# Moving bias, weighting and one sum between engines in the last two batches of a gathered attention kernel, with a new written-out order

## The chip, the core and the metric

The kernel runs on one core of a Trainium2 chip. The metric is device time in microseconds (us) of one execution. Three timed runs of the kernel before took 1618.98, 1622.75 and 1625.38 us, so the median is 1622.75 us. One further execution was recorded by the profiler: it took 1612.02 us, and its span from the first to the last instruction is 1609.9 us.

Engine names: PE is TensorE (matmul), DVE is VectorE, ACT is ScalarE, POOL is GpSimd (it also issues the indirect gathers), SP is SyncE (it only issues transfers).

## The reference

The input x has 16 batches of 1024 rows of 512 numbers. An adjacency matrix of 1024 x 1024 zeros and ones, the same for all batches, says which rows a row may look at; most rows have only a few neighbours and itself.

```
h   = max(layernorm(x), 0)
q   = h @ Wq + bq ;  k = h @ Wk + bk ;  v = h @ Wv + bv     # 8 heads of 64
s   = q.k / sqrt(64) + (0 where adj, -1e9 elsewhere)
out = x + softmax(s) @ v
```

## The kernel before

**Tiling.** The rows are sorted by their number of neighbours and cut into 8 tiles of 128 rows, t = 7 (fewest) to t = 0 (most). Per batch and tile, x is loaded, normalised (`norm`, ACT), transposed on PE (`flip`), copied to SBUF (`unflip`, ACT), multiplied by Wk and Wv (`proj_kv`, PE), copied out of PSUM (`evict_kv`) and stored to a table of K and V rows in DRAM (`store_kv`, SP). A row's K and V are then fetched slot by slot, one neighbour per slot and row, with indirect gathers (`gather`, POOL); slot 0 of a tile is the row itself and comes by a plain transfer (SP).

**Units.** The slots of a batch are worked off in 14 units u0 to u13 of 2 to 4 slots. u0 is (7,0), meaning tile 7 from slot 0; u6 is (2,0), u7 (2,3), u8 (1,0), u9 (1,4), u10 (0,0), u11 (-1,0) (further pieces of long rows), u12 (0,4), u13 (0,8). For each unit: `multiply` by q (L1298) and `score` (L1302) on DVE, `exponent` (L1306) on ACT, then each slot's V row is weighted: by `weigh_v` on DVE (one instruction, L1318), by `weigh_s` on ACT (8 instructions, one per head, L1332), or by `weigh_p` on POOL. `fold` (L1337) and `join` (L1344) sum slots on DVE or POOL; for tile 0, and for most tiles of the last batch, PE sums them in PSUM (`add_up`, L1356). `scale` divides by the row sum, `residual` (L1406) adds x, `put_out` (L1409, POOL) writes the rows. Tile 0's q is also copied to SBUF by `copy_q` (ACT, L1279), from which PE makes the q of u11 (`queries` of tile -1).

**Who adds the bias.** PE adds a bias by one more matmul into the same PSUM tile (L1055). For the V of tiles t = 7, 5, 3, 1 of every batch but the first it doesn't: DVE adds the bias while copying out of PSUM (L1073). All other copies out are ACT's (L1075).

**The order.** There is no run-time scheduling. A planner (`planned`, `Plan.ordered`) lists all operations with their engine, what each must follow and the buffers it uses. A table `PLACES` holds a number for each operation of a batch; an engine's operations are issued in the order of place plus 95.290021 times the batch number. Batches 0, 1 and 2 have tables of their own, batches 3 to 13 share one, the next to last (14) and the last (15) have `next` and `last`. `once` and `first` hold the preparation. Places only order; each engine works its list in that order and waits where something is missing. Known dependencies in the planner serve the order in which the code is written; waits on the chip come from the real uses of buffers.

**Buffers.** There are 6 gather buffers (`g`), used in turn, 2 PSUM tiles for K and V (`pkv`), 2 for q, 2 for sums (`acc`), 2 for transposes and 3 tiles for K and V on the way to DRAM. The last batch takes its units in the order 10, 11, 12, 13, 8, 6, 9, 7, 4, 3, 5, 2, 1, 0.

**Overlap of batches.** While PE makes the K and V of batch b, DVE, ACT and POOL do the attention of batch b - 1. All gathers of batch b need all eight `store_kv` of batch b.

Of the kernel before, what the change touches and what calls it, by code (L numbers as in the profile page):

```python
# [70 lines left out]
NT = len(CAPS)  # L71
BY_VECTOR = {2: 1, 3: 0, 4: 1}
ONE_MORE = ((2, 0),)
LAST_BY_VECTOR = {(2, 0): 0, (2, 3): 0, (0, 0): 0, (-1, 0): 0, (3, 0): 0, (1, 4): 0}
VECTOR_RESIDUAL = (4,)
LAST_VECTOR_RESIDUAL = (5, 4, 6, 7)
# [21 lines left out]
        list_of=(-13.2, -13.4, 13.93, 14.05, -4.33, -7.76, -9.88, 14.25,),  # L98
        tell=(-12.63, -16.97, -13.14, 9.24, 0.89, 16.11, 17.75, 19.88,),
        spread=(45.38, 47.45, 30.7, 45.48, 45.35, 30.46, 22.54, 45.26,),  # L100
        collect=(-9.17, 5.02,),
        others=(14.42,),
        perm_of=(0.42,),
        spots=(26.84,),
        long_rows=(30.4,),
        long_blocks=(16.58, 20.59, 22.61, 24.22, 24.98,),
        longest=(27.18, 29.37, 32.28, 35.43, 36.11, 39.52, 41.52, 44.79, 45.14,),
        count_pieces=(46.89,),
        first_piece=(122.72,),
        owners=(94.07,),  # L110
        flip_owners=(136.43,),
        copy_owners=(113.68,),
        list_pieces=(137.27,),
        pieces=(127.38,),
        slots=(142.24,),
        add_bias=(-19.2, -17.6,),
        spread_bias=(68.07,),
        copy_bias=(89.7,),
# [4 lines left out]
        norm=(75.49, 76.09, 77.09, 77.49, 79.89, 80.09, 80.34, 80.69,),  # L123
        flip=(75.49, 75.69, 76.49, 76.69, 78.69, 78.89, 90.39, 104.64,),
        unflip=(75.89, 76.49, 77.29, 77.89, 80.49, 80.72, 96.22, 97.88,),
        proj_kv=(75.89, 77.49, 76.29, 77.89, 76.89, 78.49, 79.09, 79.29, 86.87, 98.15, 99.79, 107.75, 135.06, 147.6, 153,
            148.32,),
        evict_kv=(76.89, 79.29, 77.69, 79.49, 78.09, 80.29, 80.4, 80.66, 96.1, 96.13, 96.42, 106.28, 154.55, 162.49, 169.71,
            172.46,),
        store_kv=(78.35, 116.17, 119.38, 125.35, 140.7, 146.55, 148.18, 147.06,),  # L130
        variance=(75.89, 76.89, 79.29, 81.69,),
        power=(75.69, 76.29, 78.29, 87.8,),
# [3 lines left out]
        load_x=(30.09, 30.5, 38.8, 45.21, 45.44, 47.92, 49.07, 49.69,),  # L136
        norm=(2.13, 2.31, 24.77, 49.09, 71.39, 77.14, 77.27, 78.66,),
        flip=(50.32, 51.95, 54.11, 55.9, 60.64, 67.45, 67.52, 68.48,),
        unflip=(27.69, 53.06, 72.64, 77.2, 79.54, 81.13, 82.77, 84.23,),
        queries=(67.49, 69.07, 115.56, 126.07, 127.49, 138.29, 148.67, 168.76, 169.97,),  # L140
        gather=(45.09, 65.92, 63.96, 81.66, 82.98, 67.8, 87.05, 86.63, 69.01, 87.14, 102.98, 103.26, 67.61, 108.86, 109.63,
            108.64, 107.92, 79.49, 116.69, 119.1, 130.36, 131.45, 130.44, 102.76, 142.21, 138.67, 142.4, 144.98, 150.63,
            142.37, 142.46, 108, 152.91, 152.09, 152.7, 153.37, 153.1, 152.82, 153.23, 171.08, 171.84, 155.19, 172.79,
            155.41, 171.17, 171.11,),
        multiply=(47.46, 64.59, 81.01, 107.03, 126.74, 113.33, 126.77, 141.63, 149.43, 155.18, 163.45, 170.22, 180.88,
            178.07,),
        score=(47.54, 67.41, 96.06, 111.76, 129.2, 117.87, 128.06, 146.83, 153.31, 155.84, 165.66, 174.39, 181.78, 195.93,),
        exponent=(92.19, 93.82, 105.44, 111.15, 115.51, 115.42, 115.56, 141.97, 143.4, 152.67, 166.31, 172.53, 173.27,
            183.23,),
        row_sums=(64.37, 70.18, 97.04, 118.27, 142.77, 160.52, 163.48, 203.64,),  # L150
        share=(64.49, 74.75, 101.56, 119.16,),
        weigh_v=(69.44, 130.54, 142.01, 144.6, 161.03, 163.57, 170.25, 175.36, 195.82,),
        weigh_s=(92.85, 101.83, 100.44, 95.75, 106.78, 112.94, 106.75, 115.48, 115.39, 115.45, 122.29, 116.89, 121.19, 119.7,
            142.94, 135.53, 142.97, 143.03, 144.58, 154.99, 152.31, 153.27, 163.13, 166.52, 165.91, 171.8, 172.93, 171.74,
            173.08, 173.04, 172.99, 174.92, 175.62, 181.86, 185.22, 185.42, 187.44,),
        fold=(71.91, 97.01, 97.07, 132.47, 137.68, 138.95, 141.69, 143.23, 145.64, 143.05, 153.79, 155.15, 156.82, 161,
            163.76, 171.2, 173.85, 175.66, 181.17, 186.5, 187.92, 183.84, 200, 202.21, 204.35, 204.53,),
        residual=(109.25, 124.53, 138.45, 141.77, 153.19, 171.14, 178.55, 219.35,),
        put_out=(129.95, 130.51, 141.35, 142.43, 153.4, 178.16, 179.5, 225.23,),
        join=(147.89, 161.06, 175.01,),  # L160
        scale=(148.16, 161.67, 176.53, 211.41,),
        copy_q=(145.23,),
        add_up=(188.54, 194.88, 203.87, 205.55,),
        more=(201.41,),
        pass_on=(203.77,),
        seen=(331.72,),
    ),
    1: dict(
        load_x=(-45.57, -43.85, -39.73, -39.1, -35.32, -8.38, 7.1, 14.11,),
        stats=(-63.36, -61.71, -54.75, -49.26, -50.34, -20.16, 1.69, 45.35,),  # L170
        norm=(-12.29, -8.07, -1.29, 11.92, 17.92, 21.28, 45.19, 45.66,),
        flip=(-14.6, 13.76, 33.62, 50.55, 65.56, 72.21, 73.87, 79.53,),
        unflip=(-6.21, -2.22, 15.4, 21.31, 28.65, 37.54, 57.61, 68.73,),
        proj_kv=(17.02, 20.04, 31.75, 42.81, 49.67, 52.6, 71.12, 55.79, 72.24, 74.1, 74.46, 79.5, 79.61, 83.24, 86.3, 90.4,),
        evict_kv=(-2.01, -35.87, 14.8, 20.07, 20.47, 37.41, 38.89, 36.39, 47.71, 60.13, 57.69, 63.79, 70.59, 76.3, 77.5,
            77.55,),
        store_kv=(7.84, 6.03, 7.72, 17.75, 21.65, 22.37, 41.88, 46.5,),
        variance=(-59.83, -48.24, 0.42, 46.54,),
        power=(-31.44, 7.33, 34.59, 50.93,),
        shift=(-56.77, -25.47, 22.23, 52.69,),  # L180
        queries=(92.98, 95.46, 99.76, 113.88, 114.01, 119.61, 134.23, 135.77, 151.42,),
        gather=(53.63, 85.6, 64.02, 85.49, 85.7, 72.03, 102.18, 95.44, 87.81, 104.49, 108.17, 108.68, 107.7, 109.8, 109.4,
            111.58, 112.73, 107.63, 119.79, 126.28, 135.9, 135.96, 135.93, 140.28, 147.73, 148, 149.33, 149.5, 150.8, 150.83,
            149.71, 142.94, 156.83, 157.14, 151.75, 157.7, 150.86, 150.89, 162.73, 165.24, 165.07, 165.98, 165.43, 166.72,
            176.54, 166.09,),
# [16 lines left out]
        scale=(164.12, 171.36, 188.49, 227.3,),  # L202
        copy_q=(144.08,),
        add_up=(188.22, 192.32, 197.88, 215.67,),
        more=(188.38,),
        pass_on=(191.08,),
        seen=(236.64,),
    ),
# [1399 lines left out]
```

## Time and profile before

| what | value |
|---|---|
| median of 3 runs | 1622.75 us (1618.98 to 1625.38) |
| the profiled execution | 1612.02 us, span 1609.9 us |
| busy, share of the span | PE 98%, DVE 94%, ACT 90%, POOL 78% |
| last store of K and V of batch 14 / 15 issued | 1410.0 / 1504.4 us |
| first gather of batch 15 | 1507.9 us |
| first multiply of batch 15 | 1524.9 us |
| last output write issued | 1603.6 us |

The span falls into three parts. Up to about 91 us the rows are sorted and the K, V of batch 0 are made. From there to 1505 us PE is fed with the K, V and q of one batch after another. From 1505 us on there are only the rest of batch 14's attention and the whole of batch 15's. Busy shares are averages over all three; the prediction reads them by stage.

### The profile page before, as it was taken

How to read it: one execution, taken by the hardware profiler on the slowest of the kernel's cores; microseconds unless marked ns; L12 is line 12 of the kernel's file. 1: busy time of each engine (PE TensorE's matmuls, PEld its weight loads, DVE VectorE, ACT ScalarE, POOL GpSimd, SP SyncE). 2: the span in 40 equal slices, each digit the busy share in tenths (PEclk: the TensorE clock that was granted, in tenths of full speed). 3: DMA queues.
4: the chain of work that ended last, by engine and by line, in shares of the span. 5: the costliest groups of instructions: out<-in, count | busy, mean ns of one | idle time of the engine just before them, and what ended most of it. 6: DMA issues, size and time to landing. Idle time of an engine off the chain costs nothing. (4 is left out here: it accounts for less than half of the span.)

```text
span 1609.9 us, 19515 instructions
## 1 busy us (share of the span) xinstructions
PE 1572.1 (98%) x4242; PEld 732.0 (45%) x4242; DVE 1518.2 (94%) x2075; ACT 1444.8 (90%) x5428; POOL 1258.7 (78%) x1185
## 2 busy tenths in 40 slices
PE   8999999999999999999999999999999999999687
PEld 4444444444444444444444444444444444444233
DVE  8889999999999999999999999999999999999897
ACT  4459999898999989899898989999998998989897
POOL 3777778887788888888788787878788887786666
PEclk9999999999999999999999999999999999999899
DMA  6499989999999999999999999999999999998886
GB/s 249 141 351 341 334 319 358 329 366 323 341 333 345 366 333 357 325 351 349 339 357 346 345 337 345 344 343 352 330 339 331 341 373 326 338 335 330 324 306 217
DMA packets 149876, 531.56 MB, mean 330 GB/s; under 512 B 19052, under 2 KB 19052, under 8 KB 149752
## 3 DMA queue, kind: packets, MB, share of 16 engines
q0 software_dynamic: 109840, 390.70, 67.9%
q1 hardware_dynamic: 39912, 139.56, 23.0%
q8 instruction: 35, 0.57, 0.1%
q14 instruction: 89, 0.73, 0.1%
HBM read 429.46 MB, written 100.72 MB: 329 GB/s over the span
## 5 line engine op out<-in xcount | busy, mean ns | idle before, releaser
L1332 ACT ACTIVATE g<-g,weights 128x64 f32<-128x64 f32 x4704 | 1160.3, 338 | 40.9 <-DVE weights L1311 37.8
L1288 POOL DMA_INDIRECT g<-kv,index x608 | 642.2, 1056 | 206.7 <-issue 163.2
L1057 PE MATMUL pq<-wq,hT 128*128 128x512 f32 x1024 | 462.4, 595 | 0.0
L1057 PE MATMUL pk<-wk,hT 128*128 128x512 f32 x960 | 431.7, 593 | 0.0
L1057 PE MATMUL pv<-wv,hT 128*128 128x512 f32 x960 | 431.4, 593 | 0.0
L1302 DVE TENSOR_REDUCE weights<-g 128x32 f32<-128x2048 f32 (+2 forms) x224 | 423.7, 1897 | 2.0
L1298 DVE TENSOR_TENSOR g<-g,pq 128x2048 f32<-128x2048 f32 (+2 forms) x208 | 388.7, 1870 | 28.1 <-DMA g<-kv 9.9
L1057 PEld LDWEIGHTS pq<-wq,hT 128*128 128x128 f32 x1024 | 195.8, 191 | 216.9 <-issue 213.2
L1057 PEld LDWEIGHTS pv<-wv,hT 128*128 128x128 f32 x960 | 182.4, 190 | 213.5 <-issue 210.6
L1057 PEld LDWEIGHTS pk<-wk,hT 128*128 128x128 f32 x960 | 182.7, 190 | 201.4 <-issue 196.8
L1337 DVE TENSOR_TENSOR g<-g 128x512 f32<-128x512 f32 (+1 forms) x301 | 253.9, 851 | 9.8 <-ACT g L1332 8.4
L1409 POOL DMA_INDIRECT out_dram<-x,perm x128 | 136.7, 1068 | 39.8 <-issue 30.6
L1002 POOL DMA_INDIRECT x<-in_x_dram,perm x128 | 135.8, 1061 | 34.9 <-issue 32.5
L1337 POOL TENSOR_TENSOR g<-g 128x512 f32<-128x512 f32 x90 | 115.0, 1284 | 17.6 <-DVE g L1337 10.5
L1037 ACT ACTIVATE h<-x,shift,rstd 128x512 f32<-128x512 f32 x120 | 96.5, 807 | 12.0 <-DVE shift L1027 11.4
L1318 DVE TENSOR_TENSOR g<-g,weights 128x512 f32<-128x512 f32 x143 | 101.9, 716 | 1.1 <-ACT weights L1306 0.6
L1356 PE MATMUL acc<-g,ident 128*128 128x512 f32 x170 | 84.4, 612 | 14.6 <-ACT g L1332 10.8
L1044 PEld LDWEIGHTS pht<-ident,h 128*128 128x128 f32 x512 | 63.2, 141 | 68.6 <-issue 52.7
L1406 POOL TENSOR_TENSOR x<-x,o 128x512 f32<-128x512 f32 x64 | 81.9, 1280 | 9.4 <-DVE o L1392 5.0
L1049 ACT COPY hT<-pht 128x512 f32<-128x512 f32 x128 | 73.0, 571 | 16.3 <-PE pht L1044 16.2
L1011 DVE BATCH_NORM_STATS2 st<-x 128x6 f32<-128x512 f32 x120 | 81.2, 677 | 1.6 <-DMA x<-in_x_dram,perm 1.6
L1044 PE MATMUL pht<-ident,h 128*128 128x128 f32 x512 | 76.5, 273 | 3.2 <-ACT hT L1049 1.9
(242 smaller groups left out, 1080.2 us busy)
## 6 DMA issues: line engine op xcount, KB each, us to landing
g<-kv SPq DMA_DIRECT2D x128, 512.0 KB, 7.7
kv<-kvt SPq DMA_DIRECT2D x120, 512.0 KB, 6.9
g<-kv,index POOLq DMA_INDIRECT x608, 6.9
adj<-in_adj_dram SPq DMA_DIRECT2D x8, 512.0 KB, 8.2
x_first<-in_x_dram SPq DMA_DIRECT2D x8, 256.0 KB, 6.0
x<-in_x_dram,perm POOLq DMA_INDIRECT x128, 5.5
out_dram<-x,perm POOLq DMA_INDIRECT x128, 6.6
wk<-in_L_gnn_Wk_dram SPq DMA_DIRECT2D x1, 1024.0 KB
```

Of the source, the lines that this page charges most:

```text
L1002: nc.gpsimd.indirect_dma_start(out=X[n][:], out_offset=None, in_=x_rows, in_offset=on(ap=perm[:, t : t + 1], axis=0), element_offset=b * N * D
L1037: nc.scalar.activation(HN[n], X[n], AF.Relu, bias=shift, scale=scale)
L1044: nc.tensor.transpose(PH[n][:, c, :], hn[:, ts(c, P)], ident)
L1057: nc.tensor.matmul(pt, HT[n][:, c, :], W[name][:, c, :], start=(apart and c == 0), stop=(n != -NT and c == DC - 1))
L1288: nc.gpsimd.indirect_dma_start(out=G[i][:, s].rearrange("p j d -> p (j d)"), out_offset=None, in_=KV[b % len(KV)][:], in_offset=on(ap=inde ...
L1298: nc.vector.tensor_tensor(k, k, Q[b, t][:, None, :].to_broadcast([P, count, D]), ALU.mult)
L1302: nc.vector.tensor_reduce(weights[:, w, :], heads(G[i][:, :count, 0, :]), AX.X, ALU.add)
L1318: nc.vector.tensor_tensor(v, v, own.to_broadcast([P, n, H, HD]), ALU.mult)
L1332: nc.scalar.activation(v[:, h, :], v[:, h, :], AF.Identity, scale=weights[:, c + s, h : h + 1])
L1337: engine.tensor_tensor(v[:, 0:n], v[:, 0:n], v[:, first : first + n], ALU.add)
L1356: nc.tensor.matmul(ACC[b, home], owner_t if t < 0 else ident, v[:, s, :], start=(u == added_up(b, B, home)[0] and s == 0), stop=(u == adde ...
L1409: nc.gpsimd.indirect_dma_start(out=out_rows[t], out_offset=on(ap=perm[:, t : t + 1], axis=0), in_=X.pop(b * NT + TILES.index(t))[:], in_of ...
```

## The change

- The V bias of the last batch is added by PE for all tiles: `LAST_BIAS_V` is empty. So four `evict_kv` (t = 7, 5, 3, 1) change from DVE with a bias to ACT as plain copies, and four bias matmuls (L1055) are added.
- In batch 14, units (2,0) = u6 and (1,0) = u8 give their DVE slot to ACT: two `weigh_v` fewer, two `weigh_s` (16 instructions) more.
- In batch 14, the `residual` of tile 4 goes from DVE to POOL.
- The planner now lets `multiply` of a tile-0 unit follow `copy_q`.
- All tables of places but the start of the preparation are new. Counted engine by engine among the operations of batches 3 to 13 that both versions have, 214 of PE's 418 stand at another position, 696 of ACT's 880, 712 of DVE's 1089 and 516 of POOL's 781; by 14, 3, 21 and 9 positions at most on ACT, PE, DVE and POOL. Order, amount and engine of the work of batches 0 to 13 are otherwise untouched.

Sorted by their new places, the operations at the passage from batch 14 to batch 15 stand so (the unit is behind the name, a slot as s0 to s3; the operations of each engine are in order):

```
ACT before: evict_kv b15 t0 V, u10 s1, u11 s0, u10 s2, exponent u12, u11 s1, u12 s1, u12 s0,
            exponent u13, u12 s2, u13 s2, u13 s1, u13 s0, copy_q 15, exponent b15 u10
ACT after:  evict_kv b15 t0 V, u10 s1, u10 s0, exponent u12, u11 s2, u12 s1, u12 s0, u12 s2, u11 s1,
            exponent u13, copy_q 15, u13 s2, u13 s0, u13 s1, exponent b15 u10
PE before:  proj_kv b15 t0 V, add_up b14 u10, pass_on 14, queries 15 0, add_up b14 u11, queries 15 -1
PE after:   proj_kv b15 t0 V, add_up b14 u10, queries 15 0, pass_on 14, add_up b14 u11, queries 15 -1
DVE before: multiply u12, join u9, scale 1, score u12, multiply u13, weigh_v u10, fold u10, fold u10,
            weigh_v u11, fold u11, more, score u13, weigh_v u12, row_sums 0, fold u12 (2 slots),
            multiply b15 u10, score b15 u10, fold u13, fold u12 (1 slot), fold u13
DVE after:  multiply u12, join u9, scale 1, score u12, fold u10, weigh_v u12, multiply u13, more, fold u10,
            weigh_v u11, score u13, fold u12 (2 slots), fold u12 (1 slot), fold u11,
            multiply b15 u10, row_sums 0, score b15 u10, fold u13, fold u13
POOL, put_out of batch 14 behind the gathers of batch 15, before: t2, t1, t5, t3, t7, t0;
            after: t5 (ahead of the gathers of u4), t3, t0, t7, t1, t2
```

At the end of the last batch, DVE's `weigh_v` of u1 moves ahead of `row_sums` of tile 7, and `residual` of tile 5 ahead of `share` of u0.

The diff, cut to its core (of the places only the rows spoken of):

```
+NEXT_BY_VECTOR = {(2, 0): 0, (1, 0): 0}
 VECTOR_RESIDUAL = (4,)
+NEXT_VECTOR_RESIDUAL = ()
...
     'next': dict(
...
-        put_out=(440.27, 176.79, 439.54, 170.01, 440.18, 349.96, 438.18, 440.42,),
+        put_out=(440.82, 165.68, 232.62, 164.09, 307.41, 515.84, 443.63, 309.64,),
-        pass_on=(220.1,),
+        pass_on=(222.73,),
...
     'last': dict(
...
-        queries=(262.15, 252.79, 252.44, 222.65, 210.97, 194.72, 156.92, 125.39, 127.47,),
+        queries=(287.36, 271.09, 242.72, 228.24, 221.53, 161.29, 160.15, 127.4, 129.47,),
-        copy_q=(115.48,),
+        copy_q=(113.62,),
...
 BIAS_V = {0: 'DVE', 2: 'DVE', 4: 'DVE', 6: 'DVE'}
+LAST_BIAS_V = {}
...
-        add(("multiply", k), "DVE", slots + [q_of[q]], [g, q])
+        add(("multiply", k), "DVE", slots + [q_of[q]] + ([("copy_q", b)] if t == 0 else []), [g, q])
...
     if b == B - 1:
         return LAST_BY_VECTOR.get(UNITS[u][:2], 1)
+    if b == B - 2 and UNITS[u][:2] in NEXT_BY_VECTOR:
+        return NEXT_BY_VECTOR[UNITS[u][:2]]
...
 def residual_by_vector(b, B, t):
-    return t in (VECTOR_RESIDUAL if b < B - 1 else LAST_VECTOR_RESIDUAL)
+    return t in (LAST_VECTOR_RESIDUAL if b == B - 1 else NEXT_VECTOR_RESIDUAL if b == B - 2 else VECTOR_RESIDUAL)
...
-def bias_by(n, name):
-
-    return BIAS_V.get(n % NT, "PE") if n >= 0 and name == "v" else "PE"
+def bias_by(n, name, B):
+
+    kinds = LAST_BIAS_V if n >= (B - 1) * NT else BIAS_V
+    return kinds.get(n % NT, "PE") if n >= 0 and name == "v" else "PE"
```

## The prediction

> **What bounds the kernel now.** I read the stretches first (busy time per engine in chosen windows; columns: window in us from the span's start, its length, busy us and instruction counts of PE, weight loads, DVE, ACT, POOL, then PE's clock, DMA share, GB/s).
>
> ```profile
> 95.00:190.00 95.00, 94.30 (x259) 44.11 (x258) 90.83 (x131) 83.45 (x314) 70.77 (x69) 1.00 0.94 344
> 475.00:570.00 95.00, 95.00 (x259) 44.35 (x258) 91.83 (x121) 89.51 (x342) 79.56 (x72) 1.00 0.94 341
> 1409.00:1505.00 96.00, 94.58 (x253) 43.35 (x251) 92.25 (x111) 87.79 (x334) 71.23 (x65) 1.00 0.91 336
> 1505.00:1525.00 20.00, 8.56 (x15) 3.20 (x16) 13.75 (x17) 19.25 (x81) 14.01 (x13) 0.71 0.82 291
> 1525.00:1610.00 85.00, 69.56 (x162) 29.84 (x161) 71.52 (x83) 65.99 (x278) 52.28 (x51) 0.94 0.74 267
> ```
>
> In the repeated batches PE has no idle time at a full clock: PE is the bound there, DVE (91.8 of 95) and ACT (89.5) follow closely. In the timeline the same step of PE comes back every 94.64 us from batch 4 to 11. The third row (K and V of batch 15) is the same regime. In the last two rows PE is no longer the bound: 105 us, of which DVE works 85.3 and ACT 85.2.
>
> Second view, the waits in 1505 to 1530 us (engine, line, what it waited for: total us, times, longest):
>
> ```profile
> PE acc L1356 <- ACT g L1332: 9.2, 1, 9.2
> ACT weights L1306 <- DVE weights L1302: 5.3, 2, 4.7
> DVE g L1298 <- ACT q L1279: 5.0, 1, 5.0
> ```
>
> Third, ACT's and DVE's timeline there (start, us, engine, line, operation, operands, then idle time before it and what ended it):
>
> ```profile
> 1516.57 0.23 ACT L1306 ACTIVATE weights<-weights 128x24 f32<-128x24 f32 x1 [0.66 <-DVE weights L1302]
> 1516.70 7.74 ACT L1332 ACTIVATE g<-g,weights 128x64 f32<-128x64 f32 x32
> 1524.34 0.56 ACT L1279 COPY q<-pq 128x512 f32<-128x512 f32 x1
> 1529.57 0.23 ACT L1306 ACTIVATE weights<-weights 128x32 f32<-128x32 f32 x1 [4.67 <-DVE weights L1302]
> ...
> 1518.73 1.23 DVE L1337 TENSOR_TENSOR g<-g 128x1024 f32<-128x1024 f32 x1 [0.86 <-ACT g L1332]
> 1524.93 2.29 DVE L1298 TENSOR_TENSOR g<-g,pq 128x2048 f32<-128x2048 f32 x1 [4.98 <-ACT q L1279]
> ```
>
> This is the one large hole: the first multiply of batch 15 has its gathers (the last landed at 1518.9) and its q (PE done 1519.8), but waits 4.98 us for `copy_q`, which stands behind four groups of weighting; then ACT waits 4.67 us for that multiply and its score.
>
> Prices, from the groups (busy total, mean ns of one, then idle before):
>
> ```profile
> L1332 ACT ACTIVATE g<-g,weights 128x64 f32<-128x64 f32 x4704 | 1160.3, 338 | 40.9 <-DVE weights L1311 37.8 <-DMA g<-kv,index 0.4 <-issue 0.2
> L1318 DVE TENSOR_TENSOR g<-g,weights 128x512 f32<-128x512 f32 x143 | 101.9, 716 | 1.1 <-ACT weights L1306 0.6
> L1055 PE MATMUL pv<-bias_parts,chosen 128*128 128x512 bf16 x60 | 22.8, 379 | 0.0
> L1073 DVE TENSOR_TENSOR kvt<-pv,bias_rows 128x512 f32<-128x512 f32 x60 | 41.0, 683 | 5.2 <-PE pv L1057 5.1
> L1075 ACT COPY kvt<-pv 128x512 f32<-128x512 f32 x60 | 34.4, 573 | 7.3 <-PE pv L1057 7.0
> L1406 POOL TENSOR_TENSOR x<-x,g 128x512 f32<-128x512 f32 x45 | 58.0, 1289 | 4.7 <-ACT h L1037 1.6 <-issue 1.6
> L1406 DVE TENSOR_TENSOR x<-x,g 128x512 f32<-128x512 f32 x16 | 10.7, 666 | 0.0
> ```
>
> **The change part by part.** The sum runs against the profiled execution, 1612.02 us (span 1609.9 plus 2.1). The median of the timed runs, 1622.75, lies 10.7 us above it; I carry this over unchanged.
>
> *Bias of V.* Four bias matmuls, 4 x 0.38 = 1.5 us on PE, all ahead of the last K and V of batch 15, in a stretch without PE slack: the last store and every gather of batch 15 come 1.5 us later. DVE loses 4 x 0.68 = 2.7 us of work, ACT gains 4 x 0.57 = 2.3.
>
> *Two slots to ACT.* DVE loses 2 x 0.72 = 1.4 us, ACT gains 16 x 1160.3/4704 = 16 x 0.247 = 3.9 us.
>
> *The sum with x.* DVE loses 0.67 us, POOL gains 1.29 in a stretch where it works 71 of 96 us, so POOL's own cost is hidden. But the timeline shows a DVE fold of two slots, otherwise 1.22 us, taking 1.97 when a POOL sum started just before it:
>
> ```profile
> 1499.60 1.29 POOL L1337 TENSOR_TENSOR g<-g 128x512 f32<-128x512 f32 x1
> 1500.01 1.97 DVE L1337 TENSOR_TENSOR g<-g 128x1024 f32<-128x1024 f32 x1
> ```
>
> So between a gain of 0.67 and a loss of 0.62 (1.29 of blocking less 0.67) on DVE. I take the gain: of 90 such folds 80 overlapped no POOL sum. The Trainium skill, "SBUF — State Buffer", section "SBUF: two separate sides", speaks against this move: a DVE operation with two SBUF inputs and a GpSimd operation that reads SBUF exclude each other for a whole instruction. That agrees with the row above; taken strictly it would make this part +0.6 rather than -0.7, and it leaves the sum as it is, since DVE does not set the passage below.
>
> Together DVE has 4.8 us less and ACT 6.2 more before the passage. ACT idles 8.0 us in 1409 to 1505, 7.1 of it before its last evictions; by 1454, 5.9 of that is gone, so of what comes later (5.6: 3.9 and three evictions) only about 2.6 fits into idle time up to 1525 (0.33, 0.51, 0.18, 0.88, 0.66). The rest can come from waits on DVE that shrink, as DVE is ahead. Likeliest is that ACT reaches its last eviction in time for PE; the bound on the other side is the rival "ACT late".
>
> *The passage, with its new order.* PE ends K and V at 1503.75 + 1.5 = 1505.25. ACT then has the eviction (0.48 to the next start), seven groups (1.91 from start to start) and two exponents (0.12 each): copy_q could start at 1505.25 + 0.48 + 13.4 + 0.24 = 1519.4, against 1524.34 with ten groups. It needs q. PE sums u10 first; u10's third group ends at about 1509.6, DVE then folds (1.2), weights (0.7), multiplies (1.7), does `more` (0.2) and folds (0.7): 1514.1, PE sums until 1516.1 and makes q until 1520.0 (4.0 us at the lowered clock, as before). That is no earlier than today: putting it ahead of `pass_on` only pays for the later fold. copy_q ends at 1520.6. Gathers: 1518.9 + 1.5 = 1520.4. DVE is at its last fold of u11 until 1520.5. So the first multiply starts at about 1521.0 instead of 1524.93: -3.9. What is queued behind copy_q: u13's three groups end at 1526.4; the score of batch 15's first unit, with 0.8 us of row sums in between, ends at 1526.3. ACT starts weighting batch 15 at 1526.6 instead of 1529.88: -3.3. The wait of `multiply` for `copy_q` is in the trace already (the 5.0 us), so its new line in the planner adds no wait.
>
> *The gathers behind it.* u8's gather waited until 1533.6 for a buffer, freed by PE's sum of batch 14's u12 (1530.79 to 1532.87), which waited for a fold that stood behind the late multiply. The fold now stands ahead of it; PE's sum of u12 then follows that of u11 (POOL's fold at 1523.5, behind gathers 1.5 later) and batch 15's second q: about 1531.0. So -2.1 for gathers. From here both chains do the same work as before (batch 15's counts are the same). Ends: -2.1 by gathers, -3.3 by ACT; I take the middle, -2.7.
>
> *Moved transfers.* Six `put_out` of batch 14 (1.07 plus 0.3 us of POOL each) change places; one now goes ahead of u4's gathers, where POOL waited 2.81 us for a buffer shortly after (before u5's), and two fewer operations stand ahead of u0's gather. Taken at 0, bounds +1.3 and -1.3. SP's stores and loads swap among neighbours; SP idles over 6 us between most of them.
>
> *The end.* A weighting (0.68) and a sum (0.67) now precede u0's share; ACT needs the share only at 1598.49, it was made at 1597.34: 1.15 of cover for 1.35. Taken at 0; +0.2 to +0.7 if the cover is gone.
>
> *Front and repeated batches.* No work changes. PE's waits at 79.1 (1.91 us) and 102.5 (0.70) bound a gain at -2.6, one more like the first a loss of +1.9; taken at 0. In the repeated batches PE has nothing to gain (one wait of 0.84 us in batches 3 to 13) and could lose; taken at 0, because PE's operations there began mostly 2 to 20 us after their inputs were ready, more than three positions usually move.
>
> Sum: +1.5 - 4.2 = -2.7 net, 1612.0 to 1609.3 in the profile's terms, 1622.75 - 2.7 = **1620.0**. By itself this lies between 1616 and 1624.
>
> **The rivals.**
>
> *ACT late.* ACT's 5.6 us after 1454 find no shrinking waits: less 1.5 (PE is later too), it reaches the last eviction up to 4.1 late, and store, gathers and copy_q move with it: -2.7 + 4.1 = +1.4, 1624.2. For it: ACT's density from 1454 on. Against: DVE is 4.8 us ahead by then.
>
> *All holes close.* DVE's idle time from 1505 on is 5.8 + 5.8 = 11.6 us; if the new order takes all, 1622.75 + 1.5 - 11.6 = 1612.7. For it: ACT has about as much idle there. Against: DMA at 0.82 share and the six buffers fix the pace of the gathers.
>
> *The shared plan of batches 3 to 13 makes PE wait (the slower side).* The tightest steps there are a flip that followed its norm by 0.45 us and a projection that followed its unflip by 0.79. If the new ACT order brings one such step late in each of 12 batches, each wait costs about the mean of the three waits of this kind in the trace (0.84, 1.91, 0.70), 1.15 us: 13.8 - 2.7 = +11.1, 1633.9. It decides from 0.9 us per batch ((8.1 + 2.7)/12). For it: 696 of 880 ACT positions changed. Against: ACT and DVE have 3 to 5 us of slack per batch, so a late step is caught up.
>
> **How the numbers follow.** Half a per cent, 8.1 us, is about what can be told from no change here (the three runs spread over 0.4%). Chances: forecast 0.42, ACT late 0.17 (both within it), all holes close 0.19 (faster), PE waits 0.22 (slower). So faster 0.19, same 0.59, slower 0.22. The range takes in 1612.7 and 1633.9 with 3 us of run spread below: 1609 to 1634; half of the slow case and a little of the fast one stay outside.
>
> **What would show it.** Right: PE still without idle in the repeated batches; last store about 1506; the 5.0 us wait for copy_q gone or under 1 us; first multiply near 1521; first exponent of batch 15 near 1526.4. Wrong: a period above 95.5 us in the repeated batches; the last store later than 1508 with PE waiting for an eviction; or the gathers of u8 still after 1533, the gain lost at the buffers.

## The result: a little slower, and the profile after

The changed kernel took 1628.03 us (median of 15 runs, 1624.17 to 1632.09), the kernel before beside it 1622.94 us (15 runs, 1618.98 to 1627.77). The ratio is 1.0031, 95% interval 1.0020 to 1.0042: +5.1 us, where the forecast said -2.7. It lies within half a per cent and inside the range, but on the other side of the forecast. On another chip, with before at 1614.83, the changed kernel, left as it is, gave 1.0050 (1.0036 to 1.0065), +8.9 us between medians.

The profiled execution after took 1630.81 us (span 1629.1). The profile of before (1612.02) was 10.9 us below its median and this one 2.8 us above, so the two profiles may not simply be subtracted; below, profiles from quieter chips are used beside them.

First view, the stretches (window, its length, busy us and instruction counts of PE, weight loads, DVE, ACT, POOL, then PE's clock, DMA share, GB/s) of the changed kernel:

```profile
320.00:370.00 50.00, 47.17 (x127) 21.59 (x126) 49.20 (x59) 44.06 (x167) 39.34 (x37) 1.00 0.94 339
490.00:585.00 95.00, 95.00 (x258) 44.34 (x257) 91.90 (x123) 89.72 (x343) 76.54 (x72) 1.00 0.94 344
1428.00:1524.00 96.00, 95.04 (x255) 43.65 (x253) 90.28 (x106) 93.13 (x359) 71.35 (x67) 1.00 0.93 333
1524.00:1544.00 20.00, 7.85 (x13) 3.44 (x13) 16.52 (x18) 17.66 (x75) 13.86 (x12) 0.74 0.76 253
1544.00:1629.00 85.00, 71.66 (x163) 30.62 (x163) 68.08 (x81) 67.63 (x287) 53.87 (x53) 0.93 0.75 275
```

The repeated batches are full of PE as before (second row). New is the first row: in batch 3 PE lacks 2.8 of 50 us, while DVE works 49.2 of 50. The tail (last two rows) has changed little: it lasts 106.1 us after PE's last projection, before 106.2.

Second view, the waits at the passage, and third, the two operations that the forecast was about:

```profile
PE acc L1360 <- POOL g L1341: 4.6, 1, 4.6
ACT q L1283 <- PE pq L1061: 2.3, 1, 2.3
DVE g L1302 <- ACT q L1283: 1.8, 1, 1.8
```

```profile
1539.60 0.58 ACT L1283 COPY q<-pq 128x512 f32<-128x512 f32 x1 [2.34 <-PE pq L1061]
...
1540.22 2.29 DVE L1302 TENSOR_TENSOR g<-g,pq 128x2048 f32<-128x2048 f32 x1 [1.81 <-ACT q L1283]
```

The 5.0 us wait for `copy_q` is down to 1.8, the first multiply of batch 15 stands 17.2 us behind PE's last projection (1523.0) instead of 21.2. So the hole closed as forecast, and the time still rose. PE now waits 4.6 us for POOL's fold of u11, before 3.5.

Fourth, the groups (busy total, mean ns of one):

```profile
L1336 ACT ACTIVATE g<-g,weights 128x64 f32<-128x64 f32 x4720 | 1163.3, 339 | 41.2 <-DVE weights L1315 30.5 <-issue 4.8 <-DVE sums L1384 1.3
L1322 DVE TENSOR_TENSOR g<-g,weights 128x512 f32<-128x512 f32 x141 | 107.5, 764 | 0.8 <-ACT weights L1310 0.4 <-ACT g L1336 0.3
L1059 PE MATMUL pv<-bias_parts,chosen 128*128 128x512 bf16 x64 | 24.3, 379 | 1.7 <-DVE kvt L1077 1.7
L1077 DVE TENSOR_TENSOR kvt<-pv,bias_rows 128x512 f32<-128x512 f32 x56 | 38.0, 678 | 14.2 <-PE pv L1061 14.2
L1079 ACT COPY kvt<-pv 128x512 f32<-128x512 f32 x64 | 36.8, 575 | 6.8 <-PE pv L1061 6.8
L1410 DVE TENSOR_TENSOR x<-x,g 128x512 f32<-128x512 f32 x15 | 10.2, 682 | 0.2
```

Counts moved as the change says. But one mean moved with no change of work: DVE's weighting (second line), 716 ns before and 764 now, two instructions fewer and 5.6 us more. That line turned out to be the key.

Last, PE's new waits in batch 3 and batch 14, with the DVE operations around the second:

```profile
355.79 0.38 PE L1059 MATMUL pk<-bias_parts,chosen 128*128 128x512 bf16 x1 [1.46 <-ACT kvt L1079]
...
360.97 1.10 PE L1279 MATMUL pq_-1_2970<-q,owner 128*128 128x512 f32 x2 [1.37 <-DVE g L1302]
...
1423.80 0.38 PE L1059 MATMUL pv<-bias_parts,chosen 128*128 128x512 bf16 x1 [1.68 <-DVE kvt L1077]
```

```profile
1418.15 2.28 DVE L1306 TENSOR_REDUCE weights<-g 128x32 f32<-128x2048 f32 x1
...
1420.86 2.29 DVE L1302 TENSOR_TENSOR g<-g,pq_-1_11952 128x2048 f32<-128x2048 f32 x1
1423.07 0.68 DVE L1077 TENSOR_TENSOR kvt<-pv,bias_rows 128x512 f32<-128x512 f32 x1
```

In batch 14 the eviction of V (1423.07) reaches PE 1.68 us late. Its place is not new: in both orders the same 1431 operations of DVE stand ahead of it, this score and this multiply among the last of them. In the profile of before it started 0.5 us behind the end of PE's projection and PE had 2.7 us to spare; here it started 4.6 us behind it. DVE came late to the whole group: it sat idle for 1.88 us before the multiply at 1414.21, and the profile does not tell what ended that wait.

### The profile page after: what moved, and what is told of

It reads as the page before. It is cut to its first block, busy times and chain, and to the rows that moved or that the text cites. A ratio compares the mean times of both kernels' runs of the same rounds, so it can differ in the third digit from the quotient of the medians.

```text
span 1629.1 us, 19502 instructions
## 1 busy us (share of the span) xinstructions
PE 1578.2 (97%) x4246; PEld 733.1 (45%) x4246; DVE 1530.9 (94%) x2068; ACT 1447.5 (89%) x5448; POOL 1245.6 (76%) x1186
## 5 line engine op out<-in xcount | busy, mean ns | idle before, releaser
L1292 POOL DMA_INDIRECT g<-kv,index x608 | 623.1, 1025 | 209.6 <-issue 156.7
L1302 DVE TENSOR_TENSOR g<-g,pq 128x1536 f32<-128x1536 f32 (+2 forms) x208 | 388.7, 1870 | 24.4 <-DMA g<-kv,index 7.5
L1006 POOL DMA_INDIRECT x<-in_x_dram,perm x128 | 140.1, 1094 | 33.7 <-issue 28.7
L1341 POOL TENSOR_TENSOR g<-g 128x512 f32<-128x512 f32 x90 | 120.2, 1337 | 25.8 <-DVE g L1341 21.1
L1322 DVE TENSOR_TENSOR g<-g,weights 128x512 f32<-128x512 f32 x141 | 107.5, 764 | 0.8 <-ACT weights L1310 0.4
L1310 ACT ACTIVATE weights<-weights 128x32 f32<-128x32 f32 (+2 forms) x224 | 49.5, 221 | 54.3 <-DVE weights L1306 49.2
```

What stands on the lines that cost most here:

```text
L1006: nc.gpsimd.indirect_dma_start(out=X[n][:], out_offset=None, in_=x_rows, in_offset=on(ap=perm[:, t : t + 1], axis=0), element_offset=b * N * D
L1292: nc.gpsimd.indirect_dma_start(out=G[i][:, s].rearrange("p j d -> p (j d)"), out_offset=None, in_=KV[b % len(KV)][:], in_offset=on(ap=inde ...
L1302: nc.vector.tensor_tensor(k, k, Q[b, t][:, None, :].to_broadcast([P, count, D]), ALU.mult)
L1322: nc.vector.tensor_tensor(v, v, own.to_broadcast([P, n, H, HD]), ALU.mult)
L1341: engine.tensor_tensor(v[:, 0:n], v[:, 0:n], v[:, first : first + n], ALU.add)
```

## The experiments

The order of the code is a list, so one order can be used up to an operation (a cut) and the other behind it, or single operations moved within it. Where the two lists are spliced, the edit is this, with the cut named each time:

```
+def plan_of(B):
+    head = first[: first.index(CUT)]          # first: one kernel's list, second: the other's
+    return head + [key for key in second if key not in head]
```

Kernels measured together ran on one chip and share the runs of before. Medians of before in the five groups: 1638.41, 1613.83, 1614.83, 1614.68 and 1613.60 us.

### Where the loss is: before again, and three splices

`same_before` is before unchanged. `new_front`: changed order up to the K and V of batch 3 (`CUT = ('proj_kv', 24, 0)`), before behind it. `new_until_14`: changed order up to `('queries', 14, 7)`, before behind it. `new_tail`: before up to that cut, the changed order and all three changed parts behind it.

> The kernel before, unchanged, as a control: how much the start of the span varies from one execution to the next. In the two profiles the K and V of batch 1 end at 175.6 us (before) and 185.4 us (after), 9.8 us apart, with one wait of PE of 6.99 us at 86.2 us in the changed kernel only. If that wait belongs to the execution and not to the order, this profile too can show its K and V of batch 1 ending well after 176 us; if it belongs to the order, it ends at 175 to 177 us again. The time is 1622.9 us within 2.

> The changed order from the start up to the K and V of batch 3, the order and the parts of before from there on. Theory 1 (the loss of 5.1 us is made by the new order of the preparation and the first batches, where the changed kernel's PE waits more often for ACT's evictions): 1626 to 1629 us. Theory 2 (the loss is made in the last two batches): 1622.9 within 1. Theory 3 (repeated batches 3 to 13 lose 0.09 us each): 1622.9 within 1.

> The changed order from the start up to the queries of batch 14, that is the front and the repeated batches; the last two batches as before, with the bias of V partly by VectorE. Theory 1 (front): 1626 to 1629 us, like the changed front alone. Theory 2 (last two batches): 1622.9 within 1. Theory 3 (repeated batches): 1624 us or more, and above the changed front alone.

> The order of before up to the queries of batch 14 (about 1417 us), from there on the changed order and all three changed parts. Theory 1 (the loss sits in the front; the 4 us gained at the first multiply of batch 15 are given back inside batch 15, so that the tail is even): 1622.9 within 1.5; the forecast's own sum, had it held, gives 1620.2. Theory 2 (the last two batches lose: 1.5 us for four bias matmuls, 1.7 us of PE waiting for an eviction, and more): 1626 to 1628 us.

Measured: 0.9985 (0.9956 to 1.0014), 1.0027 (1.0003 to 1.0050), 1.0008 (0.9987 to 1.0029), 0.9984 (0.9960 to 1.0007). This chip's runs of before spread over 1%, too much to decide. The control was still useful: here K and V of batch 1 ended at 183.9 us in before itself, with the long wait of PE near 85 us. So that wait, which stood only in the profile after, does not belong to the changed order.

```profile
84.17 1.12 PE L1044 MATMUL pht<-ident,h 128*128 128x128 f32 x4 [5.53 <-ACT hT L1049]
```

### The same on quieter chips

`same_after` is the changed kernel, unchanged; the other two are the splices just told.

> The changed kernel, unchanged, on the chip of the three runs below, so that they can be compared with it and not only with before. On a quiet chip the changed kernel with the eviction put first stood 7.3 us above before; with its own wait of 1.7 us in batch 14 left in, the changed kernel is expected at 7 to 10 us above before (ratio 1.0045 to 1.006), more than the 5.1 us measured first, because on that first chip a stall of about 7 us in the start of most executions hides a part of the new waits there.

> The changed order from the start up to the queries of batch 14, the last two batches as before: the run that gave 1.0008 with an interval of 0.4% on a chip whose runs spread over 1%. Theory 1 (the first batches make most of the loss: PE waits 9.7 us there in the changed order against 2.6 to 3 in that of before; one or two waits of 0.7 to 1.7 us more at the start of batch 14): 6 to 9 us above before, ratio 1.004 to 1.0055. Theory 2 (the last two batches make it): ratio within 0.001 of 1.

> The order of before up to the queries of batch 14, the changed order with all three parts behind it. Theory 1: the passage's gain is real on average (in six executions the changed tail ended 102.5 to 106.1 us after PE's last K and V, mean 104.5, that of before 106.2 to 108.1) and outweighs the 0.85 us of four bias matmuls: 1 to 3 us below before, ratio 0.998 to 0.9995. Theory 2 (ScalarE's extra work spoils the tail): 1 us or more above before.

Measured: `same_after` 1.0050 (1.0036 to 1.0065), `until_14_again` 1.0055 (1.0040 to 1.0070), `tail_again` 0.9991 (0.9981 to 1.0002). Theory 1 holds: the order up to batch 14, in which nothing was added or removed, costs 8.9 us (0.0055 x 1614.7); the changed tail alone gains 1.5, with an interval that just reaches nothing. Their sum, +7.4, fits the whole (8.1 by its ratio). That cut lies behind the K and V of batch 14, so the late eviction just shown belongs to the part that loses.

The profiles say where (us from the start; end of the last eviction of K and V of a batch, PE's last projection, end; worked out from the traces). The column before is the first profile of before, from the first chip. At batch 4 the six profiles of that order from quieter chips without a shortened addition lie between 459.5 and 462.5, so it can stand for them there:

| | before | tail_again | until_14_again | same_after |
|---|---|---|---|---|
| batch 3 | 368.0 | 368.1 | 375.0 | 373.9 |
| batch 4 | 461.2 | 461.2 | 469.8 | 468.8 |
| batch 13 | 1314.7 | 1316.1 | 1324.2 | 1322.8 |
| PE's last projection | 1503.7 | 1506.5 | 1516.5 | 1515.6 |
| end | 1609.9 | 1611.2 | 1622.3 | 1621.1 |
| PE's waits over 0.25 us, 100 to 470 us | 0.70 | 0.41 | 4.80 | 6.26 |

From before to `same_after`: +7.6 up to batch 4, +0.5 in batches 5 to 13, +3.8 from there to the last projection (2.0 of it waits of PE, 0.9 the bias matmuls by the price worked out below), -0.7 in the tail.

One splice misled. `new_from_3` (before up to `('proj_kv', 24, 0)`, changed behind it) was to leave the front out:

> The order of before from the start up to the K and V of batch 3, from there on the changed order and all three changed parts. Theory 1 (about 4 to 5 us of the changed kernel's loss lie in the preparation and batches 0 to 3, most of it in two waits of PE of 1.46 and 1.37 us in batch 3 and smaller ones before it): the ratio to before falls from 1.0031 to about 1.0005, that is 4 us less than the changed kernel, and the K and V of batch 3 end 94.7 to 96.5 us after those of batch 2 instead of 99.2. Theory 2 (the loss is all in the last two batches): the ratio stays at 1.003.

Measured 1.0053 (1.0040 to 1.0067). Neither: the seam made a wait of its own in batch 3, where PE waited 3.90 us for a fold of POOL, and batch 3 came 103.9 us after batch 2. Beside it the two waits of the changed order in batch 3 (1.46 and 1.37 us above) stood again, with 1.48 and 1.38 us. So it doesn't tell what the front alone costs.

### The tail: the hole, the order, the bias

`early_q`: before, with only `copy_q` moved ahead of two groups of weighting.

```
+    order = planned(B).ordered()
+    # behind ('copy_q', 15): ('weigh_s', 209, 1), ('weigh_s', 209, 0)
```

> The kernel before with one operation moved: copy_q of batch 15 goes ahead of the last two groups of weighting of batch 14 instead of behind them; nothing else of the change. If the 5.0 us hole at the first multiply of batch 15 is worth what the forecast took: the first multiply comes 3.8 us earlier against the end of K and V (17.4 instead of 21.2 us behind it), and the time falls by 2 to 4 us (ratio 0.9980). Rival (the gain is given back behind it, at the sums on PE and at the gathers, because the two delayed groups hold up the fold and the sum of unit 13): the multiply is earlier by 3.8, but the stretch from the end of K and V to the end of the span stays at 105.6 to 106.2 us, and the ratio at 1.000.

Measured 0.9971 (0.9962 to 0.9981): 1609.97 against 1613.83 us. The first multiply stands 17.6 us behind the last projection:

```profile
1520.71 0.59 ACT L1284 COPY q<-pq 128x512 f32<-128x512 f32 x1 [0.41 <-PE pq L1062]
...
1521.33 2.29 DVE L1303 TENSOR_TENSOR g<-g,pq 128x2048 f32<-128x2048 f32 x1 [1.68 <-ACT q L1284]
```

So the hole was real, and closing it by one move gives a lower ratio than the changed kernel has anywhere. `early_q_fold` also moves POOL's fold of batch 14's u11 ahead of three gathers:

```
+    # behind ('fold', 207, 1, 1): ('gather', 222, 2), ('gather', 221, 2), ('gather', 222, 0)
```

> The kernel before with copy_q of batch 15 moved ahead of two groups of weighting, as in the run that was 0.29% faster than before, and GpSimd's fold of batch 14's unit 11 moved ahead of three gathers of batch 15's unit 11 and 12, since PE waited 2.39 us for it. If that wait matters: another 1 to 2 us, ratio 0.996 to 0.9965. Rival (three gathers later by 1.3 us each cost as much as the sum gains, because the gathers of unit 13 and 8 set the pace): the ratio stays at 0.997.

Measured 0.9978 (0.9967 to 0.9990): no further gain in time. PE's sum of u11 started 16.0 us behind the last projection (19.3 in `early_q`), and then PE waited 4.72 us for the next fold, one of DVE. The rival holds for the time; its reason, the gathers, was not separated from that next wait.

`new_tail_dve_bias` is `new_tail` with `LAST_BIAS_V = BIAS_V`. `tail_order` takes before up to `('proj_kv', 127, 1)` and the changed order behind it with none of the three parts; `tail_order_bias` adds `LAST_BIAS_V = {}`.

> The order of before up to the queries of batch 14, the changed order behind it, with the two slots more on ScalarE and the sum with x on GpSimd, but with the bias of V of batch 15 as before (four evictions that add it on VectorE). If the four bias matmuls cost PE 4 x 0.38 us in a stretch that PE bounds: the K and V of batch 15 end 94.4 to 94.8 us after those of batch 14 instead of 95.4 to 96.0, and the time is 1.5 us less than with the bias by TensorE (ratio to before about 0.9975). Rival (the four additions on VectorE, 2.7 us, come back as late evictions or late multiplies): the period is 94.5, but the end of the span is no nearer to the end of K and V than 105.6 us, and the ratio is 0.9985 or more.

> The kernel before up to PE's last projection of batch 15, and the changed order behind it, with none of the three changed parts (bias, slots and sum as before). If the passage gains by its order: first multiply of batch 15 at 16 to 17.5 us behind the end of K and V instead of 21.2, the end of the span 101.5 to 103.5 us behind it instead of 106.2, and the time 3 to 4.5 us below before (ratio 0.9975). Rival (the gain of the passage needs VectorE's lighter load from the two slots and the sum): the end stays at 105 us or more behind the end of K and V, ratio 0.999 to 1.000.

> The same with the bias of V of batch 15 by four matmuls, evicted by ScalarE. From the rows a bias matmul takes PE 0.21 us more per projection (3.81 against 3.60), so K and V end 0.85 us later, not the 1.5 us of the forecast. If that is all, it stands 0.85 us above the kernel without. Rival (ScalarE is the tight engine behind the last K and V, and its evictions and weighting run late): the end of the span also moves away from the end of K and V by up to the 2.3 us of the four evictions, in sum 2 to 3 us above the kernel without.

Measured 0.9993 (0.9980 to 1.0006), 0.9990 (0.9979 to 1.0002), 0.9988 (0.9977 to 1.0000). With or without the bias on PE the time is the same within what these runs tell (0.9990 and 0.9988 on one chip; 0.9991 and 0.9993 on two): that part is not the loss, and no gain of it shows. Both first expectations were too good by 2 to 3 us. In `tail_order` the seam put weighting ahead of the last eviction, which came 2.9 us behind the last projection instead of at once, so its order is not quite that of the change.

### Why the first batches wait: place, or time lost by DVE?

`evict_first` is the changed kernel with one multiply moved behind the late eviction of batch 14:

```
+    # behind ('evict_kv', 118, 1): ('multiply', 193)
```

> The changed kernel with one operation moved: on VectorE the multiply of batch 13's unit 11 goes behind the eviction of V of batch 14's tile 1, which in the changed order stands behind it and made PE wait 1.68 us. Expected: that wait goes, the K and V of batch 14 end 95.0 to 95.6 us after those of batch 13 instead of 97.3, and the time is 1.7 to 2.3 us below the changed kernel's (ratio to before about 1.0018). Rival (VectorE is the bound there and the wait only moves to the multiply, then to ScalarE and to a later eviction): the period stays within 0.5 us of 97.3 and the ratio at 1.003.

Measured 1.0044 (1.0032 to 1.0057). The wait of 1.68 us is gone and batch 14 comes 95.7 us after batch 13 (97.3 in the first profile after, 96.3 in `same_after`). The gain in time is not resolved. (The expectation has it that this multiply stands ahead of the eviction in the changed order; it does so in before too.)

`waits_moved` also moves, in batches 1 to 3, each operation behind which PE's waits hang; `waits_moved_2` one place more:

```
+    # behind ('evict_kv', 9, 0): ('weigh_s', 2, 1)
+    # behind ('evict_kv', 19, 0): ('weigh_s', 20, 0)
+    # behind ('evict_kv', 28, 0): ('weigh_s', 35, 2), ('exponent', 36)
+    # behind ('proj_kv', 29, 1): ('queries', 2, -1)
+    # waits_moved_2, behind ('evict_kv', 28, 1): ('fold', 34, 1, 1), ('multiply', 37), ('fold', 35, 1, 1)
```

> The changed kernel with five places in its order mended by hand, each where PE waited for an eviction, or for a multiply, that stands behind weighting: the eviction of batch 14 as before (1.68 us), and K's evictions of batch 1 (0.69), batch 2 (1.05) and batch 3 (1.46) ahead of one group of weighting each, and PE's fold of unit 11 into the queries of batch 2 behind the next projection instead of ahead of it (1.37). Theory (PE is the bound from the first batch to the last K and V, so each of its waits goes into the time one to one): 5 to 6 us below the changed kernel, ratio to before 1.001 to 1.002. Rival (ScalarE and VectorE set the pace of batches 1 to 3 and the waits come back at the next eviction): less than 2.5 us below the changed kernel.

> The kernel with five places mended by hand, and a sixth: in batch 3 the waits came back as one of 3.64 us at VectorE's eviction of tile 3, which stands behind two folds and a multiply there; these three go behind it. Theory (a wait of PE in the first batches goes into the time one to one, and it is the place in the order, not VectorE's or ScalarE's load, that makes it): the waits of PE from 100 to 470 us fall from 5.9 to under 3 us, the K and V of batch 3 end 94 to 96 us after those of batch 2, and the time is 5 to 6 us below the changed kernel (ratio to before about 1.0015). Rival (load): the wait comes back a second time at a later eviction, the time stays above 1.0035.

Measured 1.0052 (1.0034 to 1.0069) and 1.0037 (1.0024 to 1.0049). In the first, the two waits of batch 3 came back as one at the next eviction, of DVE:

```profile
351.64 0.38 PE L1080 MATMUL pv<-bias_parts,chosen 128*128 128x512 bf16 x1 [3.64 <-DVE kvt L1098]
```

In the second, PE's waits between 100 and 470 us fell to 2.2 us, yet the ratio only to 1.0037, about 2 us below the changed kernel and not clear of it. Place alone does not explain the loss. Two of the late evictions, of batch 3's K (ACT, the wait of 1.46 us) and batch 14's V (DVE, 1.68 us), have the same operations ahead of them on their engine in both orders, only in another sequence. So the engines came to them late. But why, with the same work?

The answer was in the durations. In the changed kernel, DVE's weighting of 0.68 us takes up to 2.3 us in the first batches where it is under way together with an addition of POOL in SBUF. One of them (start, us, engine):

```profile
331.72 1.89 DVE L1322 TENSOR_TENSOR g<-g,weights 128x512 f32<-128x512 f32 x1
...
331.76 1.28 POOL L1410 TENSOR_TENSOR x<-x,g 128x512 f32<-128x512 f32 x1
```

DVE ends at 333.61, 0.57 us after POOL's end at 333.04. With the 0.04 us before POOL's start that is 0.61 of its usual 0.68: it stood still nearly as long as POOL added. For every DVE operation I took its duration above the median of its line, operands and shape, where that is more than 0.2 us, and summed (in `same_after` 27 of the 31, 30.6 us, lie under an operation of POOL that is no transfer; in before all 23):

| | before | tail_again | until_14_again | same_after | after |
|---|---|---|---|---|---|
| whole run, us (operations) | 16.1 (23) | 14.0 (19) | 31.5 (33) | 31.5 (31) | 33.9 (35) |
| first 400 us | 4.3 | 3.8 | 12.0 | 11.6 | 13.0 |
| 400 to 1400 us | 6.5 | 7.7 | 16.9 | 17.0 | 16.1 |

(The expectations below have 3.5 and 9.5 to 10.4 for the first 400 us; by the rule told here it is 4.3 and 11.6 to 13.0.) The same seven weightings of the first three batches come up in `after` and in `same_after`. DVE is idle for only 9 of 270 us between 100 and 370 us in `same_after`, so it has little to make up 7 us from. Is that the cause? The last row warns against a quick yes: in the repeated batches the changed order stretches DVE by 10 us more, and yet PE's waits between 470 and 1320 us grow from 0.84 to 1.15 us only. What differs is how the stretching bunches: 4.8 us between 320 and 370 us, at most 2.2 in any 50 us from 400 to 1320. The last pair takes POOL's additions away there, in both orders:

```
         def fold(i, first, n):
+            if engine is nc.gpsimd and i // NU < 4:
+                v = v[:, :, 0:1]
...
         def residual(b, t):
+            if b < 4 and not residual_by_vector(b, B, t):
+                rows, add = rows[:, 0:1], add[:, 0:1]
```

> The kernel before, with GpSimd's additions in SBUF (folds and sums with x) of batches 0 to 3 shortened to one column of 512; what these leave out of the output is wrong, the rest of the work stays. In batches 0 to 3 of before VectorE's operations that overlapped such an addition lost 3.5 us. Theory 4 (VectorE, full in the first batches, loses time to GpSimd's additions, and PE waits for it): 0 to 2 us below before, ratio 0.999 to 1.000. Rival (place in the order alone): 1.000 within 0.001.

> The changed kernel with the same shortening. There VectorE's operations lost 9.5 to 10.4 us in the first 400 us to such overlaps (3.5 in before). Theory 4: PE's waits between 100 and 400 us fall from 5.9 to under 3 us, the K and V of batch 4 end within 4 us of those of the shortened kernel before (7 to 8 us apart without the shortening), and the time is 4 to 5 us above the shortened before (ratio to before 1.002 to 1.003) instead of 8. Rival (the place of evictions and multiplies in the order makes the waits, whatever VectorE's speed): the waits of PE at about 239, 347 and 352 us stay, and the ratio stays at 1.0045 or more.

Measured 1.0004 (0.9994 to 1.0015) and 1.0010 (1.0001 to 1.0020). The changed order now stands 0.8 us above that of before (1615.78 against 1615.03) instead of 8 to 9, so more of the loss went than theory 4 had said. The K and V of batch 4 end 1.8 us apart. The stretching of the first 400 us is down to 0.2 us and 0.0, and PE's waits between 100 and 470 us in the changed order are gone without one operation moved. The stretches of `same_after`:

```profile
220.00:270.00 50.00, 48.90 (x134) 22.87 (x134) 48.27 (x57) 45.92 (x175) 39.56 (x37) 1.00 0.94 335
270.00:320.00 50.00, 49.38 (x132) 22.51 (x132) 47.91 (x63) 45.78 (x180) 39.04 (x36) 1.00 0.91 327
320.00:370.00 50.00, 47.09 (x127) 21.68 (x126) 49.40 (x55) 44.78 (x168) 38.39 (x36) 1.00 0.93 327
```

and of `after_short_pool`:

```profile
220.00:270.00 50.00, 50.00 (x138) 23.40 (x138) 47.91 (x55) 47.41 (x182) 33.86 (x38) 1.00 0.94 339
270.00:320.00 50.00, 50.00 (x137) 23.19 (x136) 46.35 (x65) 47.58 (x185) 31.00 (x38) 1.00 0.95 338
320.00:370.00 50.00, 50.00 (x137) 23.16 (x135) 49.07 (x58) 46.04 (x173) 33.81 (x36) 1.00 0.95 351
```

PE is full, and DVE does at least as much with less busy time. The group of DVE's weighting, first in `same_after`, then in `after_short_pool`:

```profile
L1322 DVE TENSOR_TENSOR g<-g,weights 128x512 f32<-128x512 f32 x141 | 107.0, 761 | 0.8 <-ACT weights L1310 0.7
```

```profile
L1322 DVE TENSOR_TENSOR g<-g,weights 128x512 f32<-128x512 f32 x141 | 98.7, 702 | 0.5 <-ACT weights L1310 0.4
```

Theory 4 is shown: POOL's additions in the first four batches make the loss in the new order and next to none in that of before. One thing stays joined to it: the shortening also gives POOL 34 us back between 100 and 370 us, so that gathers can be issued earlier. The waits speak against that as the cause. From 200 to 400 us, where PE lost 4.5 us in `same_after`, DVE waited less than 0.2 us for gathers there; and over 97 to 400 us its waits for gathers went from 6.2 to 5.2 us only, while its idle time rose (12.8 to 16.0 us) and its busy time fell. What is argued and not shown is the last step, that the bunching is what makes the same stretching cost so much in batches 1 to 3 and so little later.

## Why the prediction was wrong, step by step

- **Front and repeated batches, "taken at 0": the step that failed.** The repeated batches did cost next to nothing (+0.5 us over batches 5 to 13). The front cost +7.6 us up to batch 4, where the bounds were -2.6 and +1.9. "No work changes" was true of the count of operations but not of their time: the new places laid POOL's additions under DVE's operations, 11.6 us of stretching instead of 4.3 in the first 400 us, and DVE, idle for 9 of 270 us there, could not make it up. With these additions shortened, 0.8 us of the 8 to 9 is left. The bounds came from PE's existing waits, which cannot show an overlap that the old order does not have.
- **The sum with x.** The mechanism was in the prediction, with its row (1.22 us that took 1.97), but it was applied to the one sum that changes engine. That sum lengthened no DVE operation in the profile after: the four beside it, a multiply with q in PSUM among them, took their usual time (1.75, 0.23, 0.20, 0.64 us). Others, whose engine did not change, did. The page "SBUF — State Buffer" of the Trainium skill, section "SBUF: two separate sides", calls it an exclusive lock for a whole instruction, given to the one that starts first. The runs agree on the size: 1.28 us of POOL cost DVE 1.2 us at 331.72. They do not always agree on who waits: at 331.72 and at 1599.86 DVE's record starts first, and it is DVE that gets longer, at 1599.86 by 1.83 us, more than the addition took (see the last section).
- **Rival "the shared plan makes PE wait".** Right in sign and in what was looked for (PE waiting for late evictions), wrong in place (batches 1 to 3 and 14, not all of 3 to 13) and in cause. Its price, 1.15 us in each batch, was not seen; batches 3 to 13 are 11 and not 12, too.
- **Bias, +1.5 us on PE.** Too large. I multiplied the duration of a bias matmul, 0.38, but what counts is its start to that of the next:

```profile
336.13 0.38 PE L1059 MATMUL pq<-bias_parts,chosen 128*128 128x512 bf16 x1
336.35 3.60 PE L1061 MATMUL pq<-wq,hT 128*128 128x512 f32 x8
```

  0.22 us each, 0.9 for four.
- **"ACT late".** It did not happen: in the K and V of batch 15 (1428 to 1523 us of the profile after) PE had no wait above 0.15 us. The wait of 1.68 us lies before the changed parts, in the K and V of batch 14, and was for DVE's eviction, not for one of ACT.
- **The passage.** Forecast against the last projection (1505.25): first multiply 15.8 us behind it, u8's gather 26.3. Measured 17.2 and 27.4 in the profile after (21.2 and 29.9 before). Over eight profiles of the whole changed tail the first multiply lies at 15.8 to 17.2 us. The hole closed by 4 to 5.4 us, where 5.4 was forecast. (The -2.1 for u8's gather is 1.9 by its own ends, 1532.87 and 1531.0.)
- **"From here both chains do the same work as before."** Half wrong. In those eight profiles the end lies 102.5 to 107.0 us behind the last projection, mean 104.9; in five of the order of before it lies at 105.7 to 108.1, mean 107.0. The forecast was 102.0. About half of the gain was given back. Two things seen there may have done it; neither was tested. The last gather of u13 lands 3 to 5 us later where the trace has it (32.4 to 34.4 us behind the last projection, against 29.5 and 29.8). And DVE's weighting of batch 15's u3 lies under a sum of POOL, 2.51 us instead of 0.68 in the profile after, and at least 1.3 us too long in each of the eight changed tails:

```profile
1599.86 2.51 DVE L1322 TENSOR_TENSOR g<-g,weights 128x512 f32<-128x512 f32 x1
...
1600.53 1.29 POOL L1410 TENSOR_TENSOR x<-x,o 128x512 f32<-128x512 f32 x1
```

- **Net.** The forecast for the last two batches, -2.7, was near what they do alone (-1.5, interval -3.1 to +0.3). The sign was lost in the batches that I left out.

## What to carry to other kernels

When a whole order is written anew, the part where "only the order" changes is not free: look for a stage in which an engine is nearly full (here DVE, busy for 48 to 49 of 50 us in batches 1 to 3) and ask what the new neighbours do to its durations, and whether the long ones fall close together. Compare the mean of one instruction of the same shape before and after: a mean that rises with no change of work (716 to 764 ns) named a collision here that no view of waits showed. And a gain that hangs on one late operation is best taken by moving that one: early `copy_q` alone gave 0.29%.

## What was unexpected of the hardware

- The same kernel took 1613.6 to 1614.8 us on four occasions, 1622.9 on the first chip and 1638.4 on another.
- Near 80 us, ACT sat 7.4 to 11.5 us waiting for something that the profile does not know ("remote"), in five of the six profiles from the two chips with the longer times, in either order, and in none of the 14 from the others. The sixth is the first profile of before, the one that lay 10.9 us below its median. The line of the profile after:

```profile
83.92 0.59 ACT L1053 COPY hT<-pht 128x512 f32<-128x512 f32 x1 [11.40 <-remote]
```

  What it waits for stays open. It may be why the first chip shows +5.1 and a quieter one +8.9: a stall in the start can hide waits that the new order has there. That was not tested.
- A short operation of DVE can lose as much as a long one: one on 128x2 numbers, 0.16 us elsewhere, took 1.64 us under a sum of POOL at 356.4 us of the profile after.
- Who waits follows a pattern. In the five profiles of the table of stretching, 122 weightings, folds and joins of DVE (two inputs in SBUF) overlap an addition of POOL. Where POOL's began first, DVE's got longer (35), or neither did, with less than 0.33 us of the addition left (23). Where DVE's began first, POOL's got longer (39 of 39), unless POOL was issuing an indirect transfer when DVE's began: then it was again DVE's (21 of 25; in the other four it ended within 0.31 us of the addition's start). Such an issue alone lengthened 1 of 2204. The two rows shown above, at 331.72 and 1599.86, are of the 21.
